# Sigmoids from the half-argument tanh in a two-layer RWKV, adaLN and FP4 kernel

## The chip, the core and the metric

The kernel runs on one core of a Trainium2 chip. The metric is the device time of one execution in microseconds (us). The kernel before was timed three times: 3097.47, 3093.93 and 3090.12 us, median 3093.93 us.

## What is computed

The input is 2 sequences (B = 2) of 4096 tokens with 256 channels, all fp32. Each token goes through an adaptive layer norm, two RWKV layers (a time mix with a recurrent state, then a channel mix), a second adaptive layer norm and a feed-forward net whose operands are quantised to FP4 values. Cut to what matters here:

```python
mod = (_silu(L0_c) @ L0_wmod)                     # conditioning, once
# time mix, each of 2 layers
r = jax.nn.sigmoid(rx @ p['Wr'])
g = jax.nn.silu(gx @ p['Wg'])                     # x * sigmoid(x)
w = jnp.exp(-jnp.exp(p['time_decay'] + jnp.tanh(wx @ p['td_w1']) @ p['td_w2']))
out = _wkv(r, k, v, w, p['time_first'])           # linear in r
out = ((out - mu) / jnp.sqrt(var + EPS)) * p['gn_w'] + p['gn_b']
x = x + (out * g) @ p['Wo']
# channel mix, each of 2 layers
x = x + jax.nn.sigmoid(xr @ p['cWr']) * (k @ p['cWv'])
# feed-forward
h = jax.nn.silu(fp4_linear(x, w_gate)) * fp4_linear(x, w_up)
out = fp4_linear(h, w_down)
```

## The kernel before

**Tiles.** A sequence is cut into 16 tiles of 256 tokens, so there are 32 tiles, 64 passes of time mix (`time_mix`, L988) and 64 of channel mix (`channel_mix`, L1126), and 64 feed-forward chunks of 128 tokens (`ffn_chunk`, L1342). A tile of activations is a "slot" of 128 partitions by 512 fp32. A feed-forward chunk is a "long" of 128 by 704, whose gate and up halves are 352 columns each. Products go to five PSUM "banks" of 128 by 512. A bank is handed out when a step's first matmul is placed and comes free after its last reader (`bank`, `close`).

**Streams.** Each sequence has one stream for layer 1 and one for layer 2. Further streams hold the feed-forward inputs, the feed-forward weights, the conditioning and the last three tiles' chunks (`FFN_TAIL = 3`). Each is a Python generator that records instructions.

**Who sets the order.** No engine order is written out by hand. The class `Plan` (L118) takes the recorded instructions of all streams, gives each a cost from a formula (`weight`, L422) and a change-over cost from `TURN` (L138) wherever its `form` (L411) differs from that of the instruction before it on its engine, and picks at each step the ready instruction that could start first, older ones first within 40 ns (`SOON`) on the same engine (`run`, L342). For TensorE the form is the shape of the array in use, with 94 ns a change. For ScalarE it is Sigmoid or Exp, with 1283 ns a change; Tanh, Copy, Square and the like have no form. The order so found is then issued as it is, and every engine runs its list in that order. The recorded calls all bear the line L294 in the profile, so groups are told apart by tile names and shapes.

**The places that the change touches.** `time_mix` makes the gate g (L1034 to L1039): Wg product to a bank, Sigmoid from the bank on ScalarE, then VectorE multiplies by the bank. It makes r (L1063 to L1065): Wr product, then a Sigmoid into the first half of `rk_s`, the r rows; k follows into the second half. `wkv` (L845) holds a lock, so that one head computation runs at a time. It begins with `with_bonus` on ScalarE (L857), which reads r and k, and ends with the group norm over heads (L977), whose scale is the power -1/2 of mean square plus EPS. `time_mix` then multiplies by g and adds the Wo product to h (L1121). `channel_mix` makes sigmoid(cWr product) (L1150), multiplies it by the cWv product (L1155) and adds it to h (L1157). `ffn_chunk` makes sigmoid(gate), gate times it, and the product with up (L1355, L1356, L1362), in two halves. `conditioning` does silu of the condition once (L1167).

Of the kernel before, what the change touches and what calls it, by code (L numbers as in the profile page):

```python
# [13 lines left out]
AF = mybir.ActivationFunctionType  # L14
ALU = mybir.AluOpType
# [5 lines left out]
J = D // P  # L21
TT = 256
C = TT // P
HS = 64
# [7 lines left out]
EPS = 1e-5  # L32
# [85 lines left out]
class Plan:  # L118
# [16 lines left out]
    SAME = {"vector": 84.0, "scalar": 25.0, "gpsimd": 80.0}  # L135


    TURN = {"tensor": 94.0, "scalar": 1283.0}  # L138

    def after(self, o, op):  # L140
        return o.end + (self.SAME.get(o.eng, 0.0) if o.eng == op.eng else self.LAT[o.eng] + self.SEEN.get(op.eng, 35.0))
# [11 lines left out]
    def begin(self, seed, dry):  # L153

        self.dry, self.random = dry, random.Random(seed)
        if not self.stocks[0][1]:
            for q in self.stocks:
                q[1] = list(q[0])
        for q, tiles in self.stocks:
            q[:] = tiles  # L160
        self.banks = [(0.0, b) for b in self.all]
        self.seen = {t: [q] for t, q in self.loads.items()}
        self.held = dict.fromkeys(self.held, 0)
        self.free = {e: 0.0 for e in self.ENG}
        self.lock = {"vector": 0.0, "gpsimd": 0.0}
        self.form = {"tensor": None, "scalar": None}
        self.cur = None
        self.count = 0

# [241 lines left out]
def form(eng, fn, out, ins, a):  # L411
    if eng == "tensor":
        return (ins[0].shape[0], P if fn == "transpose" else out.shape[0])
    if eng == "scalar" and fn == "activation" and a[2] in (AF.Sigmoid, AF.Exp):
        return a[2]


def is_dram(v):
# [41 lines left out]
def rwkv_adaln_fp4_kernel(ctx: ExitStack, tc: tile.TileContext, a: dict, out: bass.AP):  # L460
# [68 lines left out]
    pl = Plan(nc, banks)  # L529
# [14 lines left out]
    def give(*ts):  # L544
        stock.extend(ts)
# [13 lines left out]
    cT = const.tile([P, J, B], F32, name="cT")  # L559
# [193 lines left out]
    def by_chunk(t):  # L753
        return t.rearrange("p c j t -> p j c t")

    def chunks(ps):
        return ps.rearrange("p j (c t) -> p j c t", c=C)
# [87 lines left out]
    def wkv(i, b, rk_s, dec_s, v_s):  # L845
# [128 lines left out]
                give2(rk_s)  # L974
            yield

        pl.vector.tensor_scalar(rs, rs, 1.0 / HS, EPS, ALU.mult, ALU.add)  # L977
        pl.gpsimd.tensor_tensor(rs, rs, nhalf[:, :n], ALU.pow)
        pl.vector.tensor_tensor(
            o_sb.rearrange("p c (h v) -> p (c h) v", v=HS), po.rearrange("p c (h v) -> p (c h) v", v=HS),  # L980
# [7 lines left out]
    def time_mix(i, b, h):  # L988
# [45 lines left out]
        bk, pg = proj(w["Wg"], v3(xg_s))  # L1034
        g_s = xg_s
        g_t = v3(g_s)
        pl.scalar.activation(g_t, pg, AF.Sigmoid)
        pl.vector.tensor_tensor(g_t, g_t, pg, ALU.mult)
        pl.close(bk)  # L1039
        yield  # L1040
        bk, pd = pl.bank()
# [19 lines left out]
            for m in range(2)  # L1061
        )
        bk, o = proj(w["Wr"], v3(xr_s))  # L1063
        pl.scalar.activation(by_chunk(r_t), chunks(o), AF.Sigmoid)
        pl.close(bk)  # L1065
        give(xr_s)
        yield
        bks, os = zip(*(pl.bank() for _ in range(2)))
# [49 lines left out]
        give(g_s)  # L1118
        yield
        bk, o = proj_tok(w["Wo"], [oT[:, k, :] for k in range(J)])  # L1120
        pl.vector.tensor_tensor(h, h, o, ALU.add)  # L1121
        pl.close(bk)
        give(oT_s)
        yield
# [1 line left out]
    def channel_mix(i, b, h):  # L1126
        w = lay[i]
        x, sx, x_s, sx_s = yield from shifted(h, w["ln2_w"], carry[i][b][1])
        xk, xk_s = lerp(x, sx, w["ck_maa"])
        xr, xr_s = lerp(x, sx, w["cr_maa"], sx_s)  # L1130
        give(x_s)
        yield
        kks = []
        for g in range(FD // P // 2):
            bk, o = pl.bank()
            o = halves(o)
            for m in range(2):
                n0 = (2 * g + m) * P
                for k in range(J):
                    mm(o[:, m, :], w["cWk"][:, k, n0 : n0 + P], xk[:, k, :], k == 0, k == J - 1)  # L1140
            kks.append(take_slot() if g < FD // P // 2 - 1 else xk_s)
            kg = v3(kks[-1])
            pl.scalar.activation(kg, o, AF.Relu)
            pl.close(bk)
            pl.scalar.activation(kg, kg, AF.Square)
            yield
        sr_s = xr_s
        sr = v3(sr_s)
        bk, o = proj_tok(w["cWr"], [xr[:, k, :] for k in range(J)])
        pl.scalar.activation(sr, o, AF.Sigmoid)  # L1150
        pl.close(bk)
        yield
        kk = [v3(u)[:, m, :] for u in kks for m in range(2)]
        bk, o = proj_tok(w["cWv"], kk)
        pl.vector.tensor_tensor(sr, sr, o, ALU.mult)  # L1155
        pl.close(bk)
        pl.vector.tensor_tensor(h, h, sr, ALU.add)  # L1157
        give(sr_s, *kks)
        yield

# [2 lines left out]
    def conditioning():  # L1163

        few = pl.take(tiny)
        cs = few[:, : J * B].rearrange("p (k b) -> p k b", k=J)
        pl.scalar.activation(cs, cT, AF.Sigmoid)  # L1167
        pl.vector.tensor_tensor(cs, cs, cT, ALU.mult)
        wide_s, tmp_s = take_slot(), take_slot()
        lnb = lnw[:, :D]  # L1170
        wide = v4(wide_s)
        for b in range(B):
            pl.vector.tensor_copy(wide[:, b, :, :], cs[:, :, b].unsqueeze(2).to_broadcast([P, J, P]))
        yield
        for g, (n0, n1) in enumerate((("sa", "ca"), ("ga", "sb"), ("cb", "gb"))):
            for b in range(B):
                bk, pm = pl.bank()
                for k in range(J):
                    mm(pm, wide[:, b, k, :], wmod[k, g][:, :512], k == 0, k == J - 1)
                for h, nm in enumerate((n0, n1)):  # L1180
                    src, dst = pm[:, h * D : (h + 1) * D], rows[nm][b]
                    if nm in ("ca", "cb"):
                        pl.vector.tensor_scalar(dst, src, 1.0, None, ALU.add)
                    elif nm in ("sa", "sb"):
                        pl.vector.tensor_copy(dst, src)
                    else:

                        sgn, mag = tmp_s[:, :D], tmp_s[:, D : 2 * D]
                        pl.vector.tensor_scalar(sgn, src, 0.0, 2.0, ALU.is_ge, ALU.mult)
                        pl.scalar.activation(mag, src, AF.Abs)  # L1190
                        pl.vector.tensor_scalar(mag, mag, 0.25, None, ALU.max)
                        pl.vector.scalar_tensor_tensor(dst, sgn, -1.0, mag, ALU.add, ALU.mult)
                        if nm == "ga":
                            pl.vector.tensor_tensor(dst, dst, lnb, ALU.mult)
                pl.close(bk)
                known.update(((n0, b), (n1, b)))
                yield
            give(*(wmod[k, g] for k in range(J)))
        give(wide_s, tmp_s, lnw)
        tiny.append(few)  # L1200
# [141 lines left out]
    def ffn_chunk(c, b, t, x1_s, xq_s, left):  # L1342
        HF = FI // 2
        cs_ = slice(c * P, (c + 1) * P)
        x1, xqT = v3(x1_s), v3(xq_s)
        while not long:
            yield
        hb_s = pl.take(long)
        hb = hb_s[:, :FI]
        for s in range(2):  # L1350
            fs = slice(s * HF, (s + 1) * HF)
            bk, gp = pl.bank()
            for k in range(J):
                mm(gp[:, :HF], xqT[:, k, cs_], wg[:, k, fs], k == 0, k == J - 1)
            pl.scalar.activation(hb[:, fs], gp[:, :HF], AF.Sigmoid)  # L1355
            pl.vector.tensor_tensor(hb[:, fs], hb[:, fs], gp[:, :HF], ALU.mult)  # L1356
            pl.close(bk)
            yield
            bk, up = pl.bank()
            for k in range(J):  # L1360
                mm(up[:, :HF], xqT[:, k, cs_], wu[:, k, fs], k == 0, k == J - 1)
            pl.vector.tensor_tensor(hb[:, fs], hb[:, fs], up[:, :HF], ALU.mult)  # L1362
            pl.close(bk)
            yield
        while not long:
            yield
        p_s = pl.take(long)
        yield from fp4(pl, hb_s, FI, P, scales[1 + c], p_s)
        long.append(p_s)
        hT_s = hb_s  # L1370
        hT = hT_s.rearrange("p (f n) -> p f n", f=NF)
        for g in range(2):
            bk, pt = pl.bank()
            for f in range(3):
                at0 = f_at[3 * g + f]
                tr(pt[:, f * P : (f + 1) * P], hb[:, at0 : at0 + P])
            pl.scalar.copy(
                hT[:, 3 * g : 3 * g + 3, :], pt[:, : 3 * P].rearrange("p (f n) -> p f n", f=3)
            )
            pl.close(bk)  # L1380
            yield
        bk, y = pl.bank()
        for f in range(NF):
            mm(y[:, :D], hT[:, f, :], wd[:, f, :], f == 0, f == NF - 1)
        ob_s = take_slot()
        ob = ob_s[:, :D]
        pl.vector.tensor_tensor(ob, y[:, :D], rows["gb"][b], ALU.mult)
        pl.close(bk)
        long.append(hT_s)
        yield  # L1390
        pl.gpsimd.tensor_tensor(ob, ob, x1[:, c, :], ALU.add)
        pl.sync.dma_start(out=rows_of(out, b, t)[:, c, :], in_=ob)
        give(ob_s)
        left.append(c)
        if len(left) == C:
            give(xq_s, x1_s)
        yield
# [75 lines left out]
```

## Time and profile before

| what | value |
|---|---|
| median of three runs | 3093.93 us |
| lowest, highest | 3090.12, 3097.47 us |
| span of the profiled execution | 3081.1 us |
| median run less that span | 12.8 us |
| PE busy in the span | 2920.0 us (95%) |
| VectorE (DVE) busy | 2345.6 us (76%) |
| ScalarE (ACT) busy | 1667.6 us (54%) |
| GpSimd (POOL) busy | 1015.7 us (33%) |
| ACT table loads | 115, 147.5 us |

The span runs from the first to the last instruction of one profiled execution; the page gives no other time for that execution, and what lies around its span is read as the difference to the median run. A row of a group gives its engine and operation, the tiles written and read, the shape, the count, the busy time with the mean ns of one, and the idle time of the engine just before with what ended it. PE is the matmul side of TensorE, PEld its weight loads. Each fp32 matmul of the program shows as two PE records. Granted clock is the share of full speed that TensorE was given.

### The profile page before, as it was taken

The page shows a single profiled execution, that of the slowest core. Times are in us where ns is not written, and L with a number is a line of the kernel's source. Part 1 is how long each engine was busy: PE and PEld are TensorE (multiplying, and loading weights), DVE is VectorE, ACT ScalarE, POOL GpSimd, SP SyncE. Part 2 cuts the span into 40 slices and gives each one's busy share as a digit, 9 for nine tenths or more (in the row PEclk, how much of TensorE's full clock was granted, in tenths as well). Part 3 has the DMA queues.
Part 4 walks back from the last instruction along what each step waited for, and adds up shares of the span by engine and source line. Part 5 has one row for each costly group of instructions (what it writes and reads, how often), then busy time and mean ns, then how long its engine had stood idle before and what let it go on. Part 6 is the DMA issues. An engine that isn't in the chain of part 4 may idle for free. (4 is left out here: it accounts for less than half of the span.)

```text
span 3081.1 us, 89987 instructions
## 1 busy us (share of the span) xinstructions
PE 2920.0 (95%) x38460; PEld 2388.7 (78%) x38460; DVE 2345.6 (76%) x6146; ACT 1667.6 (54%) x3478; POOL 1015.7 (33%) x1208
## 2 busy tenths in 40 slices
PE   6899999999999999999999999999999989999997
PEld 4678788777788887888778787787878778787775
DVE  6687876877787877878587777777778776777777
ACT  3465655564565656555564645646456454645452
POOL 2343333333333342333334233242323323232320
PEclk8899999999999999999999999999999999999999
DMA  4000000000000000000000000000000000000000
GB/s 141 12 19 9 15 7 16 3 16 7 13 12 4 20 3 13 11 8 15 5 18 4 10 13 4 19 5 19 4 8 15 3 20 3 6 11 9 9 14 11
DMA packets 35728, 42.56 MB, mean 14 GB/s; under 512 B 2816, under 2 KB 33536, under 8 KB 35328
## 3 DMA queue, kind: packets, MB, share of 16 engines
q1 hardware_dynamic: 35328, 36.81, 3.7%
q8 instruction: 302, 4.95, 0.6%
q14 instruction: 98, 0.80, 0.1%
HBM read 28.41 MB, written 8.39 MB: 12 GB/s over the span
## 5 line engine op out<-in xcount | busy, mean ns | idle before, releaser
L294 POOL TENSOR_TENSOR slot<-slot,slot 128x256 f32<-128x256 f32 (+1 forms) x768 | 578.1, 780 | 819.1 <-DVE slot L294 615.2
L294 ACT ACTIVATE slot<-bank 128x512 f32<-128x512 f32 (+2 forms) x644 | 334.3, 521 | 594.5 <-PE bank L294 563.4
L294 POOL TENSOR_TENSOR tiny<-tiny,nhalf 128x2 f32<-128x2 f32 (+1 forms) x288 | 296.9, 1034 | 874.6 <-DVE tiny L294 852.3
L294 PE MATMUL bank<-slot,cWk 128*128 128x256 f32 x1536 | 364.3, 385 | 4.5 <-DVE slot L294 4.5
L294 PE MATMUL bank<-slot,small 32*128 32x256 f32 (+3 forms) x2816 | 354.9, 359 | 10.3 <-DVE slot L294 6.9
L294 PE MATMUL bank<-cWv,slot 128*128 128x256 f32 x1536 | 342.4, 379 | 0.0
L294 PEld LDWEIGHTS bank<-slot,cWk 128*128 128x128 f32 x1536 | 288.1, 192 | 50.4 <-DVE slot L294 6.5
L294 ACT ACTIVATE slot<-bank,small 128x256 f32<-128x256 f32 (+1 forms) x640 | 250.9, 453 | 138.8 <-PE bank L294 128.7
L294 PEld LDWEIGHTS bank<-cWv,slot 128*128 128x128 f32 x1536 | 290.5, 190 | 39.7 <-issue 0.3
L294 PEld LDWEIGHTS bank<-slot,small 32*128 32x128 f32 (+3 forms) x2816 | 248.5, 178 | 86.2 <-issue 33.9
L294 DVE TENSOR_TENSOR slot<-slot,bank 128x512 f32<-128x512 f32 x192 | 130.7, 681 | 227.2 <-PE bank L294 193.5
L294 DVE TENSOR_TENSOR slot<-slot,slot 128x512 f32<-128x512 f32 x320 | 229.2, 718 | 82.2 <-PE pa L294 46.1
L294 DVE SCALAR_TENSOR_TENSOR slot<-bank,small,slot 128x256 f32<-128x256 f32 x640 | 265.1, 474 | 16.3 <-PE bank L294 16.0
L294 POOL TENSOR_TENSOR slot<-slot 128x512 f32<-128x512 f32 x128 | 140.3, 1098 | 358.4 <-ACT slot L294 253.5
L294 PEld LDWEIGHTS pa<-slot 64*32 64x32 f32 x11264 | 143.5, 109 | 79.9 <-DVE diag L294 35.2
L294 PE MATMUL pa<-slot 64*32 64x16 f32 x11264 | 171.6, 193 | 33.9 <-DVE diag L294 18.8
L294 PE MATMUL bank<-ident,slot 128*128 128x128 f32 x1152 | 176.1, 280 | 22.3 <-DVE slot L294 14.1
L294 DVE SCALAR_TENSOR_TENSOR slot<-slot,small,slot 128x256 f32<-128x256 f32 x384 | 183.4, 516 | 14.9 <-POOL slot L294 14.8
L294 ACT ACTIVATE slot<-slot 128x512 f32<-128x512 f32 x288 | 182.4, 636 | 21.9 <-DVE slot L294 17.3
L294 ACT ACTIVATE slot<-slot,tiny 128x256 f32<-128x256 f32 x256 | 141.6, 596 | 93.3 <-DVE tiny L294 89.9
L294 PE MATMUL bank<-wd,long 128*128 128x256 f32 x768 | 183.0, 389 | 2.2 <-ACT long L294 2.2
L294 PEld LDWEIGHTS bank<-ident,slot 128*128 128x128 f32 x1152 | 136.0, 143 | 57.8 <-DVE slot L294 19.6
(110 smaller groups left out, 5718.7 us busy)
## 6 DMA issues: line engine op xcount, KB each, us to landing
slot<-in_L_attn_x_dram SPq DMA_DIRECT2D x64, 256.0 KB, 2.8
out_dram<-slot SPq DMA_DIRECT2D x64, 128.0 KB, 1.7
slot<-in_L_wmod_dram SPq DMA_DIRECT2D x6, 256.0 KB, 7.7
cWk<-in_L_attn_cWk_dram SPq DMA_DIRECT2D x2, 768.0 KB, 8.1
cWv<-in_L_attn_cWv_dram SPq DMA_DIRECT2D x2, 768.0 KB, 9.4
small<-in_small_dram SPq DMA_DIRECT2D x2, 718.0 KB, 8.4
long<-in_L_ffn_w_down_dram SPq DMA_DIRECT2D x2, 352.0 KB, 2.8
long<-in_L_ffn_w_gate_dram SPq DMA_DIRECT2D x5, 128.0 KB, 2.2
```

Source lines behind the costliest of these rows:

```text
L294: fn(*[real(v) for v in a], **{n: real(v) for n, v in k.items()})
```

## The change

Each Sigmoid becomes a Tanh of half the argument, by sigmoid(x) = (1 + tanh(x/2)) / 2. The one and the half are put into VectorE instructions that follow, by turning a tensor_tensor (two inputs) into a scalar_tensor_tensor (a constant and two inputs). For r, twice the sigmoid is kept: a new ScalarE Copy with bias 1 adds the one in place, and as the head's output is then doubled, the group norm's EPS is multiplied by 4. The gate g is kept doubled as well, and the half is put into the addition of the Wo product. The conditioning gets one further small VectorE instruction. The scheduler's ScalarE change-over cost and form go. With that the planner gives another order on every engine.

```diff
-    TURN = {"tensor": 94.0, "scalar": 1283.0}
+    TURN = {"tensor": 94.0}
...
-        self.form = {"tensor": None, "scalar": None}
+        self.form = {"tensor": None}
...
 def form(eng, fn, out, ins, a):
     if eng == "tensor":
         return (ins[0].shape[0], P if fn == "transpose" else out.shape[0])
-    if eng == "scalar" and fn == "activation" and a[2] in (AF.Sigmoid, AF.Exp):
-        return a[2]
...
-        pl.vector.tensor_scalar(rs, rs, 1.0 / HS, EPS, ALU.mult, ALU.add)
+        pl.vector.tensor_scalar(rs, rs, 1.0 / HS, 4.0 * EPS, ALU.mult, ALU.add)
...
-        pl.scalar.activation(g_t, pg, AF.Sigmoid)
-        pl.vector.tensor_tensor(g_t, g_t, pg, ALU.mult)
+        pl.scalar.activation(g_t, pg, AF.Tanh, scale=0.5)
+        pl.vector.scalar_tensor_tensor(g_t, g_t, 1.0, pg, ALU.add, ALU.mult)
...
-        pl.scalar.activation(by_chunk(r_t), chunks(o), AF.Sigmoid)
+        pl.scalar.activation(by_chunk(r_t), chunks(o), AF.Tanh, scale=0.5)
         pl.close(bk)
+        rows_r = rk_s[:, : J * TT]
+        pl.scalar.activation(rows_r, rows_r, AF.Copy, bias=1.0)
...
-        pl.vector.tensor_tensor(h, h, o, ALU.add)
+        pl.vector.scalar_tensor_tensor(h, o, 0.5, h, ALU.mult, ALU.add)
...
-        pl.scalar.activation(sr, o, AF.Sigmoid)
+        pl.scalar.activation(sr, o, AF.Tanh, scale=0.5)
...
-        pl.vector.tensor_tensor(sr, sr, o, ALU.mult)
+        pl.vector.scalar_tensor_tensor(sr, sr, 1.0, o, ALU.add, ALU.mult)
         pl.close(bk)
-        pl.vector.tensor_tensor(h, h, sr, ALU.add)
+        pl.vector.scalar_tensor_tensor(h, sr, 0.5, h, ALU.mult, ALU.add)
...
-        pl.scalar.activation(cs, cT, AF.Sigmoid)
+        pl.scalar.activation(cs, cT, AF.Tanh, scale=0.5)
+        pl.vector.tensor_scalar(cs, cs, 0.5, 0.5, ALU.mult, ALU.add)
...
-            pl.scalar.activation(hb[:, fs], gp[:, :HF], AF.Sigmoid)
-            pl.vector.tensor_tensor(hb[:, fs], hb[:, fs], gp[:, :HF], ALU.mult)
+            pl.scalar.activation(hb[:, fs], gp[:, :HF], AF.Tanh, scale=0.5)
+            pl.vector.scalar_tensor_tensor(hb[:, fs], hb[:, fs], 1.0, gp[:, :HF], ALU.add, ALU.mult)
...
-            pl.vector.tensor_tensor(hb[:, fs], hb[:, fs], up[:, :HF], ALU.mult)
+            pl.vector.scalar_tensor_tensor(hb[:, fs], hb[:, fs], 0.5, up[:, :HF], ALU.mult, ALU.mult)
```

## The prediction

> **What bounds the kernel.** I read the busy times first, then the windows, then who PE waited for, then ACT's groups, then the timeline around table loads.
>
> ```profile
> PE 2920.0 (95%) x38460; PEld 2388.7 (78%) x38460; DVE 2345.6 (76%) x6146; ACT 1667.6 (54%) x3478; POOL 1015.7 (33%) x1208
> ```
>
> TensorE is the bound. Its 95% is not mere overlap: in the timeline, eight 128x256 records of one group start every 0.215 us (1.89 us for eight of 385 ns each), so the array streams. (The Trainium skill, "Trainium Kernel Development and Optimization", Quick Reference, calls matmul busy time a bad metric because matmuls are pipelined and would look at weight loads, here 78%; by that rule a fifth of the span would be open, but the start-to-start times leave only what follows.) Cut into start, middle and end:
>
> ```profile
> 0.00:200.00 200.00, 155.44 (x2146) 119.32 (x2148) 139.05 (x403) 87.61 (x190) 60.21 (x93) 0.87 0.19 64
> 200.00:2960.00 2760.00, 2665.11 (x35874) 2192.46 (x35870) 2112.16 (x5538) 1542.04 (x3216) 935.70 (x1095) 0.99 0.03 10
> 2960.00:3081.10 121.10, 99.44 (x447) 76.97 (x445) 94.36 (x206) 37.96 (x73) 19.84 (x20) 0.95 0.04 12
> ```
>
> The columns are window, length, busy PE, PEld, DVE, ACT, POOL, then the clock. PE is idle 44.6 us at the start, 94.9 in the middle (3.4%) and 21.7 at the end. Anything ACT gives must come out of these 161 us, and out of the clock that is lost after gaps (at 1523 us, after gaps of 1.6 and 0.9 us, eight Wg records take 3.57 us instead of 1.89). What ended PE's waits in the middle:
>
> ```profile
> PE bank L294 <- DVE slot L294: 18.4, 26, 1.7
> PE pa L294 <- DVE diag L294: 17.6, 24, 1.9
> PE bank L294 <- ACT slot L294: 15.2, 18, 2.4
> ...
> PE kv L294 <- ACT slot L294: 6.4, 11, 1.4
> ...
> PE pa L294 <- ACT attn L294: 3.9, 6, 1.5
> ```
>
> ACT ends about 30 us of them (15.2, 6.4, 3.9, and two smaller, 3.5 and 1.2), VectorE some 48.
>
> **Table loads.** ACT's row:
>
> ```profile
> L294 ACT ACT_TABLE_LOAD x115 | 147.5, 1283 | 26.2 <-PE bank L294 15.3 <-DVE masks L517 7.1 <-DVE long L294 1.1
> ```
>
> The built program after the change has 1 load instead of 115, at the start. In the trace a load has 18 ns before and 12 ns behind it, and other back-to-back ACT instructions overlap by 92 ns, so one load costs ACT 1283 + 18 + 12 + 92 = 1405 ns, and 114 cost 160 us. (The skill's page "ScalarE: Activation LUTs", What ACT_TABLE_LOAD costs, puts a switch at 2.66 us with a drain; by that it would be 303 us. No drain stands beside the loads in this trace, so I take the row.) How much of the 160 us does PE feel? One load, as the timeline has it:
>
> ```profile
> 1526.83 1.28 ACT L294 ACT_TABLE_LOAD   x1 [4.20 <-PE bank L294]
> 1527.21 0.44 PE L294 MATMUL bank<-S,slot 128*128 128x128 f32 x2
> 1527.49 0.56 PE L294 MATMUL bank<-slot,attn 128*128 128x64 f32 x4
> ...
> 1527.88 0.50 PE L294 MATMUL bank<-ident,long 128*128 128x128 f32 x3
> 1528.13 0.87 ACT L294 ACTIVATE slot<-bank 128x512 f32<-128x512 f32 x2
> ...
> 1528.22 1.89 PE L294 MATMUL bank<-slot,small 128*128 128x256 f32 x8
> 1528.76 0.69 DVE L294 TENSOR_TENSOR slot<-slot,bank 128x512 f32<-128x512 f32 x1 [0.38 <-ACT slot L294]
> ```
>
> ACT had idled 4.20 us before it, VectorE waits 0.38 us for the sigmoid behind it, and PE runs on with other streams. I did this for all: 106 loads start between 200 and 2960 us; in the 5 us from the start of each, PE idles 22.9 us in sum, where 3.44% of 530 us would be 18.2 by chance. The excess, **4.7 us**, is what I take off. From 8 to 20 us after a load PE idles 84.2 us against 43.7 by chance, 40 us more. That may be the loads' long shadow, or only that an Exp comes ahead of the head computation, where PE's waits lie anyway (130 of the idle us fall between a head's first bonus copy and its last state update). Heads with two to four loads inside them show no more idle PE (1.6 to 2.2 us) than those with one (2.5 us), so I take the second reading and keep 40 us for the range.
>
> At the start 8 loads (at 50.3 to 197.5 us) go in a phase where PE idles 22% and little lies beside the chain: 8 x 1.4 = 11.2 us at most, nothing at least; I take half, **5.6 us**.
>
> **What is added to ACT.** 64 copies with bias over 128x512. The nearest row, ACT slot<-slot 128x512, has a mean of 636 ns, 544 net of overlap, so 35 us. ACT's net is 125 us less; Tanh of a half is costed like the Sigmoid (596 ns is the mean of the bank-to-slot row, which holds Tanh and Relu as well). The copy lies on the path from the Wr product to the head: in the new written order it stands 1 to 3 instructions behind the Tanh, and in 42 of 64 heads the first bonus copy follows it within 4. So the head's start is up to 0.64 us later, nothing where ACT or the lock waits anyway. The lock makes heads follow each other; 64 of 35.2 us median are 2250 of 3081 us, so this chain is not the bound, and I take 0, upper end 64 x 0.64 = 41 us. (The skill's page on ScalarE, Rules for kernel authors, says adds belong on VectorE; by rows 443 against 636 ns, 12 us less work, but on the engine that is 76% instead of 54% busy, so this gives no term.)
>
> **VectorE.** 448 two-input instructions become scalar_tensor_tensor: 192 over 128x512 (681 and 718 ns before; rows of the new kind have 684 and 694: nothing) and 256 over 128x352 (514 ns before). The new kind is not in the trace at 352. At 256, the constant form has 419 (ga<-slot) against 420 ns for two inputs from a bank, the form with a per-partition scalar 474. So 0 to 54 ns each, 0 to 14 us of VectorE; the nearest row says about 0. VectorE-ended waits of PE are 48 us beside 2112 busy, 2%, so even 14 us reach PE as under 1 us. I add **0.5**. The small extra one in the conditioning is 0.2 us, once.
>
> **The order.** Counted in the two programs, PE changes its array shape 998 times instead of 969. A change from 128x256 records to a 64-row product takes 309 ns start to start instead of 216, 93 more: 29 x 0.093 = **2.7 us** more. At the end, the PE work written behind the last cWv product rises from 112 matmuls (44.1 us, by 0.216, 0.296 and 0.109 us a record) to 164 (67.0 us): feed-forward work was kept for the end.
>
> ```profile
> 3035.29 1.35 PE L294 MATMUL bank<-wu,slot 128*128 128x352 f32 x4
> 3042.02 1.12 PE L294 MATMUL bank<-ident,slot 128*128 128x128 f32 x4 [5.38 <-DVE slot L294]
> ...
> 3067.25 1.54 PE L294 MATMUL bank<-ident,long 128*128 128x128 f32 x6 [6.83 <-DVE long L294]
> ```
>
> The first wait, for the last tile's quantisation, now has work to cover it: **5.4 us** less. The second, for the last chunk's, stays. Whether the rest of the new order is better or worse is not to be had from the trace; the middle's 94.9 us bound it on the good side.
>
> **Sum.** -4.7 - 5.6 + 0 + 0.5 + 2.7 - 5.4 = -12.5 us. Span 3081.1 to 3068.6, and with the 12.8 us that the median run lies above the span, **3081 us**, 0.4% faster. A difference under 0.2% (6 us) can't be told from none here.
>
> **Rivals.**
> 1. The long shadow is real (0.17): loads delayed chains, and PE starved 8 to 20 us later. For: 84 against 44 us. Against: heads with more loads idle no more. Another 40 us off: 3041 us.
> 2. Cover everywhere (0.15): PE works while ACT loads, and start, order and end come out even: 3094 us, within 6. For: ACT idles for PE far longer than loads take. That the loads stay cannot be: the program has one.
> 3. Slower, by the copy on r's path (0.23). In 42 heads the bonus copy stands right behind it, inside the only serial chain, and PE's waits for the pa products are there. It gives up to +41 us; with the savings, up to 3122, at half the price 3102. It decides from 12.5 / 0.64 = 20 heads that pay in full.
>
> **Chances.** Forecast 0.45 (own range 3070 to 3090), rivals 0.17, 0.15, 0.23. Range 3041 to 3112: it takes in rival 1 and leaves out the far part of rival 3, 0.1, and about 0.05 in cases not thought of on either side. Faster by over 0.2% (below 3087.7): most of the forecast and rival 1, 0.57. Same 0.19, slower (above 3100.1) 0.24.
>
> **What would show it.** Right: one load; ACT about 1540 us busy; PE busy near 2920, idle of the middle near 90; the 5.4 us wait near the end gone. If idle of the middle falls below 60, rival 1; if head stages show more ACT-ended waits for rk and the middle idles over 110, rival 3. Wrong altogether if scalar_tensor_tensor at 352 takes over 600 ns or PE's lost clock changes by more than 10 us.

## The result and the profile after

The change made the kernel slower. Five runs of it have a median of 3106.76 us, five of the kernel before 3091.19 us; the ratio is 1.006, 95% interval 1.0034 to 1.0087. The forecast was 3081 us and faster. The time lies inside the stated range, but on the other side of no change. The profiled execution has a span of 3101.7 us, against 3081.1 us. In all the runs that give both, an execution takes 1.7 to 2.1 us longer than its span. So the 12.8 us that the text ahead takes for what lies around the span are mostly something else: the profiled execution of the kernel before took about 3083 us, less than any of its five timed ones, and the 20.6 us between the spans stand for 15.6 us between the medians.

The busy times of the page, in the order of the line shown for the kernel before:

```profile
PE 2933.5 (95%) x38460; PEld 2391.0 (77%) x38460; DVE 2354.3 (76%) x6147; ACT 1560.9 (50%) x3428; POOL 1012.5 (33%) x1208
```

ACT is 107 us less busy: 146 us of loads have gone, and 39 us of copies have come. Of the groups by shape, these are the ones that the change was costed by: ACT's loads after, and VectorE's feed-forward products before and after.

```profile
L294 ACT ACT_TABLE_LOAD x1 | 1.3, 1283 | 7.0 <-DVE masks L515 7.0
```

```profile
L294 DVE TENSOR_TENSOR long<-long,bank 128x352 f32<-128x352 f32 x256 | 131.1, 514 | 63.9 <-ACT long L294 41.2 <-PE bank L294 19.6
L294 DVE SCALAR_TENSOR_TENSOR long<-long,bank 128x352 f32<-128x352 f32 x256 | 131.8, 515 | 72.5 <-ACT long L294 53.0 <-PE bank L294 16.7
```

One load is left, and the form with a constant and two inputs takes 515 ns where the form with two inputs took 514. So VectorE's changed instructions did not become dear. The windows (length, busy PE, PEld, DVE, ACT, POOL, clock, DMA share, GB/s) say where the 20.6 us of the span are:

```profile
0.00:200.00 200.00, 157.22 (x2192) 121.99 (x2192) 143.42 (x417) 87.16 (x203) 64.00 (x98) 0.87 0.19 64
200.00:2960.00 2760.00, 2664.56 (x35838) 2185.53 (x35837) 2112.73 (x5530) 1436.47 (x3157) 930.96 (x1093) 0.99 0.04 10
2960.00:3102.00 142.00, 111.67 (x434) 83.45 (x434) 98.12 (x201) 37.24 (x70) 17.58 (x18) 0.87 0.03 11
```

They are to be held beside the windows of before in the prediction. The middle is the same: PE idles 95.4 us there, before 94.9, although ACT was freed of 106 us in it. By 2960 us PE has done about the same work (434 records are left, before 447), but these take 142 us instead of 121, at a clock of 0.87 instead of 0.95. What ended PE's waits in the middle has changed though its sum has not. First the line of before for GpSimd, then the lines of after:

```profile
PE bank L294 <- POOL slot L294: 8.5, 10, 3.2
```

```profile
PE bank L294 <- DVE slot L294: 20.5, 24, 4.1
PE bank L294 <- POOL slot L294: 15.7, 16, 2.1
PE pa L294 <- DVE diag L294: 10.6, 15, 1.4
PE kv L294 <- ACT slot L294: 9.5, 17, 1.3
...
PE bank L294 <- ACT slot L294: 3.5, 9, 0.7
```

ACT-ended waits for banks fell from 15.2 to 3.5 us, and GpSimd's rose from 8.5 to 15.7. The end, in PE's timeline:

```profile
3000.74 0.82 PE L294 MATMUL bank<-ident,long 128*128 128x128 f32 x6
...
3008.05 1.35 PE L294 MATMUL bank<-wu,slot 128*128 128x352 f32 x4
3019.04 1.54 PE L294 MATMUL bank<-ident,long 128*128 128x128 f32 x6 [9.64 <-DVE long L294]
...
3040.80 1.54 PE L294 MATMUL bank<-ident,long 128*128 128x128 f32 x6 [4.23 <-DVE long L294]
...
3062.02 0.63 PE L294 MATMUL bank<-ident,slot 128*128 128x128 f32 x4 [1.07 <-DVE slot L294]
3065.78 1.11 PE L294 MATMUL bank<-ident,long 128*128 128x128 f32 x6 [3.13 <-DVE long L294]
...
3092.16 0.87 PE L294 MATMUL bank<-ident,long 128*128 128x128 f32 x6 [3.98 <-DVE long L294]
```

Four times PE stands still for over 3 us until VectorE has quantised a chunk, and once for 1.1 us for a tile. Before there were two waits of over a microsecond behind the last cWv, of 5.4 us for a tile and 6.8 us for a chunk.

### The profile page after: what moved, and what is told of

It is laid out like the page before. It is cut to its first block, busy times and chain, and to the rows that moved or that the text cites. A ratio compares the mean times of both kernels' runs of the same rounds, so it can differ in the third digit from the quotient of the medians.

```text
span 3101.7 us, 89885 instructions
## 1 busy us (share of the span) xinstructions
PE 2933.5 (95%) x38460; PEld 2391.0 (77%) x38460; DVE 2354.3 (76%) x6147; ACT 1560.9 (50%) x3428; POOL 1012.5 (33%) x1208
## 4 chain that ended last, share of the span: by engine, by line
PE 69%; DVE 18%; ACT 9%; issue 2%; POOL 1%; POOLq 0%; ACTq 0%; DVEq 0%
PE bank L294 63%; DVE slot L294 9%; PE pa L294 5%; ACT slot L294 4%; DVE long L294 4%; ACT rk L294 2%; ACT attn L294 2%; DVE tiny L294 2%; DVE rk L294 1%; DVE diag L294 1%; DVE scales L294 1%; PE kv L294 1%; POOL slot L294 1%; DVE S L294 0%; ACT long L294 0%
## 5 line engine op out<-in xcount | busy, mean ns | idle before, releaser
L294 PE MATMUL bank<-slot,small 32*128 32x256 f32 (+3 forms) x2816 | 364.3, 362 | 15.1 <-DVE slot L294 11.9
L294 DVE SCALAR_TENSOR_TENSOR slot<-slot,bank 128x512 f32<-128x512 f32 x128 | 87.6, 684 | 226.3 <-PE bank L294 204.8
L294 ACT ACTIVATE slot<-slot 128x512 f32<-128x512 f32 x352 | 221.2, 631 | 32.5 <-DVE slot L294 25.8
L294 DVE TENSOR_TENSOR slot<-slot,slot 128x512 f32<-128x512 f32 x256 | 185.3, 724 | 62.4 <-PE pa L294 31.6
L294 PE MATMUL bank<-wd,long 128*128 128x256 f32 x768 | 189.4, 399 | 1.3 <-ACT long L294 1.0
L294 DVE SCALAR_TENSOR_TENSOR long<-long,bank 128x352 f32<-128x352 f32 x256 | 131.8, 515 | 72.5 <-ACT long L294 53.0
L294 PE MATMUL bank<-wg,slot 128*128 128x352 f32 x512 | 177.7, 470 | 3.5 <-DVE slot L294 2.2
```

What stands on the lines that cost most here:

```text
L294: fn(*[real(v) for v in a], **{n: real(v) for n, v in k.items()})
```

## The experiments

Ratios are to the kernel before, timed beside the variant on the same chip, with the 95% interval. Differences between two variants are worked out from their ratios times 3091 us.

**Split the change into its instructions and its order.** The theory (E) was that the written order of the end costs the time and that loads and arithmetic hardly matter to PE. Rival C was the copy on r's path, rival L a long shadow of the loads. The first run issues the change's instructions in the old order: the planner keeps its reckoning, and the copy rides with the Tanh ahead of it.

```diff
-    TURN = {"tensor": 94.0}
+    TURN = {"tensor": 94.0, "scalar": 1283.0}
...
+    if eng == "scalar" and fn == "activation" and (a[2] == AF.Exp or a[2] == AF.Tanh and k.get("scale") == 0.5):
+        return a[2]
...
-        pl.scalar.activation(rows_r, rows_r, AF.Copy, bias=1.0)
+        pl.cur.queue[-1].calls.append((nc.scalar.activation, (rows_r, rows_r, AF.Copy), {"bias": 1.0}))
```

> All instructions of the change, issued in the very order of the kernel before: the planner reckons the Tanh of a half as it reckoned the Sigmoid, and the added copy and the small one of the conditioning ride along with the instruction beside them at no reckoned cost. PE, GpSimd and SyncE run the same list as before; ACT has 1 table load instead of 115, and 64 copies more. Theory E (the written order of the end costs the time, the loads were hidden): 3075 to 3092 us, 0 to 0.5% faster than the kernel before. Rival C (the copy on r's path, or the three-operand form on VectorE, costs it): 3100 us or more, as the kernel after. Rival L (the loads have a long shadow that the new order hides): about 3050 us.

Measured: 3077.51 us, ratio 0.9953 (0.9938 to 0.9967): **0.47% faster**, 14.5 us. The second run is the mirror: the old instructions in the new order, that is, in a planner without the table changes and with the copy planned and not issued.

```diff
+        pl.scalar.activation(rows_r, rows_r, AF.Copy, bias=1.0)
+        pl.cur.queue[-1].calls.clear()
```

> The Sigmoids and two-operand instructions of the kernel before, issued in the very order of the kernel after; ACT has 101 table loads again and no copy on r's path. Theory E: 3105 to 3122 us, as slow as the kernel after or a little slower by the loads. Rival C: 3085 to 3095 us, as the kernel before. Rival L: 3140 us or more.

Measured: 3165.57 us, ratio 1.024 (1.0224 to 1.0256). So in the new order the arithmetic is worth 1.024 less 1.006, 1.8% or 56 us. The page's busy line of this run, and its middle window:

```profile
PE 2956.0 (93%) x38460; PEld 2402.3 (76%) x38460; DVE 2354.0 (74%) x6146; ACT 1651.4 (52%) x3464; POOL 1013.8 (32%) x1208
```

```profile
200.00:2960.00 2760.00, 2632.38 (x34836) 2154.02 (x34835) 2063.69 (x5411) 1487.88 (x3125) 916.19 (x1074) 0.98 0.03 10
```

ACT is only 52% busy, and still PE has idled 32 us more in the middle than in the kernel after (127.6 against 95.4) with the same PE list, and done 1002 records less. Theory E had 3105 to 3122 us for this: it falls in that the loads are not cheap. In the order of before they cost little, in one that doesn't allow for them much. The first run also gives the bill of the kernel after: its instructions in the old order -0.47%, then the new order with equal instructions 1.006 / 0.9953, **+1.1% or 33 us**.

**The copy alone.** The kernel after, its copy recorded in the plan and not issued (`calls.clear()` behind it, as above), so that r is off by one.

> The kernel after in its own order, without the 64 copies that add one to the r rows (r is then off by one, so this part of the computation is changed). Theory E: 3103 to 3108 us, no difference to the kernel after. Rival C: 3095 us or less, the copies give back at least 12 us.

Measured: 3099.01 us, 1.0025 (1.0016 to 1.0035). Against 1.006 that is 0.35%, 11 us by ratios and 8 by medians, with intervals that just touch. So the copies cost something near a quarter of their 41 us, known only roughly, and not the whole loss.

**The end.** Two kinds of run were made for theory E. The first gives the last eight tiles' feed-forward precedence in the kernel after.

```diff
+            if n >= B * NT - 8:
+                pl.cur.late = -1.0
             b, t, x1_s = done.pop(0)
...
+            pl.cur.late = -1.0
             yield from ffn_chunk(c, *ready[c].pop(0))
```

> The kernel after, with the feed-forward of the last eight tiles given precedence in the planner, so that PE's list is the same up to instruction 17663 of 20018 and 21 us of PE work instead of 67 stand behind the last cWv product. Theory E (the feed-forward kept for the end is paced by VectorE): the stretch behind the last cWv shrinks from 101 us to about 60, and the time is 3085 to 3096 us. If the end is slow for another reason (the clock, or the arithmetic): 3104 us or more.

Measured: 3130.76 us, 1.0131 (1.0114 to 1.0149), the wrong way. The stretch behind the last cWv product did shrink, from 100.8 to 48.3 us, but PE's timeline shows the waits ahead of it and in it:

```profile
3045.21 1.11 PE L294 MATMUL bank<-ident,slot 128*128 128x128 f32 x4 [7.22 <-ACT slot L294]
...
3093.13 1.12 PE L294 MATMUL bank<-ident,slot 128*128 128x128 f32 x4 [11.89 <-DVE slot L294]
```

It seems that the feed-forward that had filled PE while the last heads ran was used up. In any case, less work left for the end did not make the kernel faster. The second pair takes the quantisation of the last three tiles' chunks off VectorE, in the kernel after and, as a control, in the kernel before.

```diff
-            yield from ffn_chunk(c, *ready[c].pop(0))
+            yield from ffn_chunk(c, *ready[c].pop(0), tail=True)
...
-        yield from fp4(pl, hb_s, FI, P, scales[1 + c], p_s)
+        yield from fp4(NoVector if tail else pl, hb_s, FI, P, scales[1 + c], p_s)
```

`NoVector` records the VectorE instructions in the plan and doesn't issue them, so that these chunks are not quantised.

> The kernel after in its own order; in the six feed-forward chunks of the last three tiles the eight VectorE instructions that quantise the 704 columns are not issued (this part of the computation is left out). That is 6 x 5.8 = 35 us of VectorE less, and none of PE. Theory E (VectorE paces the end): the stretch behind the last cWv product shrinks from 101 us to 75 to 85, the time to 3082 to 3092 us. If the order's loss lies in PE's own clock or in array shape changes: not under 3101 us.

> The control: the same VectorE instructions not issued in the kernel before, in its own order (the same part of the computation is left out). Its end has 63 us of VectorE left for 60 us of PE work, where the kernel after has 78. Theory E: it gains less, 6 to 12 us, mostly the 6.8 us wait before the last chunk: 3079 to 3086 us. If it gains as much as the kernel after does from the same cut, the end of the new order is not specially VectorE's.

Measured: 3096.8 us, 1.0021 (1.001 to 1.0031), so 12 us less than the kernel after; and 3073.09 us, 0.9949 (0.9931 to 0.9967), 16 us less than the kernel before. The end behind the last cWv, in the windows of the kernel after and of its cut, then of before and its cut:

```profile
3000.90:3101.70 100.80, 72.41 (x269) 51.22 (x266) 77.44 (x154) 22.38 (x43) 11.40 (x12) 0.86 0.03 11
```

```profile
3010.30:3095.40 85.10, 66.66 (x268) 47.65 (x266) 47.30 (x106) 21.79 (x43) 9.15 (x12) 0.91 0.04 13
```

```profile
3018.30:3081.10 62.80, 45.23 (x180) 32.90 (x178) 44.31 (x87) 14.72 (x28) 7.25 (x8) 0.91 0.04 13
```

```profile
3023.70:3071.30 47.60, 41.05 (x180) 30.06 (x178) 22.61 (x51) 13.89 (x28) 6.04 (x8) 1.00 0.05 17
```

Both ends shrink by 15 us and stay 38 us apart. This VectorE work costs either end about as much: as an account of the difference, theory E falls here by its own test. What the windows do show is 88 PE records more behind the last cWv (268 against 180, 21 us at their start-to-start times), and 17 us more in which PE idles (28.4 against 17.6 us) or has less clock (0.86 against 0.91).

**The planner.** Next, the reckoning alone: the Sigmoids of before, a planner that doesn't see the loads.

```diff
-    TURN = {"tensor": 94.0, "scalar": 1283.0}
+    TURN = {"tensor": 94.0}
...
-    if eng == "scalar" and fn == "activation" and a[2] in (AF.Sigmoid, AF.Exp):
-        return a[2]
```

> The Sigmoids of the kernel before, with the table change taken out of the planner's reckoning and nothing else changed: 117 loads that the planner doesn't see. Theory P (the loads were cheap because the planner allowed for them, and cost about 0.6 us each where it doesn't): 3120 to 3165 us. Rival (the order at the end is all): 3085 to 3110 us.

Measured: 3164.98 us, 1.0244 (1.0222 to 1.0266). That agrees with theory P, but is one order only. The opposite, the change's instructions with the planner still reckoning 1283 ns at each change of function (the two pieces of the first run's edit that are shown first, with the copy planned as an instruction of its own):

> The instructions of the kernel after, with the planner still reckoning 1283 ns at each change between Exp and the Tanh of a half, and planning the 64 copies; 1 load. 25 us of PE work stand behind its last cWv, against 67 in the kernel after and 44 in the kernel before. Theory E: 3075 to 3098 us, better than the kernel after, since no feed-forward is kept back. Rival (any order planned without regard to real loads is as good as the kernel after's, and the end doesn't matter): 3104 to 3110 us.

Measured: 3096.66 us, 1.0017 (1.0004 to 1.003). That lies in theory E's range, near its upper end, and outside its rival's, so this run alone speaks for E. The run differs from the first one only in that the planner knows of the 64 copies and the small instruction of the conditioning, and yet is 0.64%, 20 us, slower. So a small change in what the planner sees moves the time by as much as the whole change did. That suggested a third theory (D): the order is a draw, worth tens of us, and the kernel before had a good one. The planner gives each instruction a rank, its place in the order of recording plus a random number of up to 8 (`op.age + self.random.uniform(0.0, JITTER)`), and takes lower ranks first. The 8 are places in that order; the expectations below call them ns, which is wrong. Other draws are at hand:

```diff
-    best = min(range(PLANS), key=lambda seed: plan(seed, True))
+    plan(1, True)
+    best = 1
```

> The kernel after, with another draw of the planner's small random tie-breaks (up to 8 ns of rank per instruction), nothing else. 44 us of PE work stand behind its last cWv. Theory D (the draw of the order is worth tens of us, and the kernel after had an ordinary or poor one): somewhere in 3070 to 3130 us, clearly apart from 3107. Theory R (a planner without the table changes gives worse orders as such): 3100 to 3115 us.

> As the run before, a second other draw, with 32 us of PE work behind the last cWv. Theory D: 3070 to 3130 us and apart from the first draw by over 10 us. Theory R: 3100 to 3115 us.

> The kernel after with a third other draw of the tie-breaks; 57 us of PE work behind the last cWv. The three draws so far gave 3107, 3079 and 3115 us. Theory D: 3070 to 3125 us, below the two other draws of the kernel before (3122 and 3150 us). If it lies above 3122 us, the change is not faster over draws either.

> The kernel before, with another draw of the same tie-breaks; 121 loads. Theory D (and the kernel before had a good draw): 3095 to 3135 us. Theory R (the planner that reckons with table changes gives good orders): 3085 to 3098 us.

> As the run before, a second other draw; 125 loads. Theory D: 3095 to 3135 us. Theory R: 3085 to 3098 us.

And the pair of instructions in these two other old orders, made as in the first run:

> All instructions of the change in the very order of the kernel before's first other draw (3121.7 us with its Sigmoids and 121 loads). Theory F (a fixed price of the 114 to 124 loads less the copies, as in the order of the kernel before): 3103 to 3111 us. Theory V (the price of the loads depends on how far the order allows for them: poor orders are poor because the loads hurt there): 3065 to 3095 us.

> The same in the order of the second other draw (3150.4 us with its Sigmoids and 125 loads). Theory F: 3131 to 3140 us. Theory V: 3075 to 3120 us.

All ratios are to the kernel before, which is draw 0 of the old planner with Sigmoids:

| order | with Sigmoids | with Tanh of the half |
|---|---|---|
| old planner, draw 0 | 1 (the kernel before) | 0.9953 (0.9938 to 0.9967) |
| old planner, draw 1 | 1.0091 (1.0065 to 1.0118) | 1.0025 (1.0011 to 1.004) |
| old planner, draw 2 | 1.0187 (1.0168 to 1.0206) | 1.0151 (1.0128 to 1.0174) |
| new planner, draw 0 | 1.024 (1.0224 to 1.0256) | 1.006 (1.0034 to 1.0087; the kernel after) |
| new planner, draw 1 | | 0.9952 (0.9934 to 0.9971) |
| new planner, draw 2 | | 1.007 (1.0048 to 1.0092) |
| new planner, draw 3 | | 1.0109 (1.0083 to 1.0136) |

Read along a row, the order is fixed, and the change's instructions are faster every time: by 0.5, 0.7, 0.4 and 1.8%. Read down a column within one planner, the instructions are fixed and the random part of the rank moves the time by up to 1.9% with Sigmoids, and by 2.0% (old planner) and 1.6% (new planner) with Tanh. The kernel before is the best of its planner's three draws, by 0.9%; the kernel after is the second of four, hardly apart from the third. Both take draw 0 because only one plan is made (`PLANS` is 1), so this was luck and not choice. The mean of the old planner's Sigmoid draws is 1.0093, that of the new planner's Tanh draws 1.0048. So theory D holds in the main (its range for the old planner's draw 2 ended at 3135 us, and 3150 were measured), and theory R (one planner as such gives the better orders) does not: its 3085 to 3098 us for the old planner's other draws were missed by 24 and 52 us. The pairs in the other two old orders were to tell a fixed price of the loads (F) from one that varies with the order (V): draw 1, with 3097.18 us, lies between V (up to 3095) and F (from 3103), and draw 2, with 3131.53 us, in F. So within the old planner's orders the gain is much the same, 11 to 20 us, each known to within 5 to 10 us; the one order planned blind to the loads that has its pair pays several times as much for them.

Two of these beat both kernels: the change's instructions in the old order (3077.51 us) and the kernel after with draw 1 (3079.14 us).

Where the order's time lies can be narrowed by one more count in the traces. Let every PE record weigh the median start-to-start time of its group, so that PE's list has the same weight in every run, and look at the last 100 us of it. They begin at 2950 us in the kernel before and at 2951 in the kernel after, and take 131 and 151 us: nearly all of the 20.6 us lie there. In the first run they begin at 2945 and take 133. In the other runs that leave nothing out, the feed-forward run aside, they begin between 2930 and 3020 and take 141 to 160. So the order of the kernel before has the shortest end of all, but the orders differ at least as much ahead of the end: of the new planner's four draws with Tanh, these 100 us begin between 2930 and 2976 and take 145 to 160.

## Why the prediction was wrong

**Table loads: right in sign, too small.** The sum took off 4.7 us in the middle and 5.6 at the start. In the same order the whole arithmetic gave 14.5 us, copies included; if these cost 8 to 11 us there as in the new order, the loads were worth some 22 to 26. The 5 us window behind a load was the mis-sized step: in the new order with its Sigmoids the same count of PE's idle time gives 31.6 us against 20 by chance, an excess of 12 us, where that run has 42 us more of idle PE than the kernel after in the whole (210 against 168 us) and is 56 us slower, although it has no copies. So most of what the loads cost falls outside that window. The 40 us of excess from 8 to 20 us behind a load, put aside as chance of place, may hold a part of it. The reading that heads with more loads inside show no more idle PE says nothing of loads ahead of a head.

**The copy: 0 was too low, the bound held.** In the new order it is 8 to 11 us of a possible 41. Rival 3 named the right side for a wrong reason: without the copies the kernel after is still 0.25% slower than before.

**VectorE: right.** 515 against 514 ns, nothing.

**The end: wrong.** "The first wait, for the last tile's quantisation, now has work to cover it: 5.4 us less" failed as a gain. That wait did shrink, to 1.1 us. But the PE work added behind the last cWv is feed-forward, each chunk of which has to come back through VectorE, so there were more waits for chunks (9.6, 4.2, 3.1 and 4.0 us, before 6.8) and less clock (0.86, before 0.91). The stretch grew by 38 us for 21 us of work. The prediction's 44.1 and 67.0 us of PE work there are too high: a transpose shows as one record, not two, which makes them 39.3 and 60.4.

**The order: the step that decided.** "Whether the rest of the new order is better or worse is not to be had from the trace; the middle's 94.9 us bound it on the good side." There was no bound on the bad side, and 2.7 - 5.4 us, a small gain, stood for the order in the sum. It measured +33 us at equal instructions, against the 14.5 us that the instructions gave in the old order. PE's lost clock rose by 10 us as well (59 to 69 us), the mark that the prediction had set for being wrong altogether. The profile of one execution can't show that the order before was a good draw of its planner; only other draws could.

**What stays open.** Why a given draw ends or fills worse is not settled; that the kernel after loses its time in the end says where, not why. Both attempts to tell it by the end (precedence, and the cut with its control) went against the theory they were made for. Whether the new planner's orders are better on the whole than the old one's is not shown by four and three draws. That the loads cost so much in the new order because the planner didn't reckon with them, and not because that one order is tender to any delay of ACT, is likely from the first two runs but was not tested on a second blind order with its pair.

## What to carry to other kernels

Where a planner or scheduler writes the order, an edit is two edits, its instructions and a new draw of the order. Measure each with the other held fixed, and take several draws before a difference of a per cent is put down to the instructions. An engine that is 54% busy can still cost the bound engine time, by delay: what 160 us of loads cost PE here, net of the copies that replace them, was 11 to 56 us, and was largest in the one order that had been made without them in mind.

## What the runs showed of the hardware

Two executions with the same PE list can differ by more than their waits, because less clock was granted where PE waited. In the end of the kernel after, six records of one shape take 1.54 us behind the wait of 9.64 us, at a clock of 0.50, and 0.82 us ahead of it. When VectorE work was left out of the end, so that PE waited less, the clock there rose from 0.91 to 1.00 (kernel before) and from 0.86 to 0.91 (kernel after). The mean clock was 0.981 in the profiled run of the kernel before, 0.978 in that of the kernel after and 0.973 in that with Sigmoids in the new order. Times the spans, with the clocks unrounded, 59, 69 and 84 us of PE's clock were not granted, so of the 64 us between the last two spans some 15 are lost clock rather than waiting. The five runs of the kernel after spread from 3103.3 to 3123.2 us, and the two slowest of them have the two lowest clocks (0.974 and 0.972).
